# The order of the work behind the last unit of a Perceiver layer: quads taken two at a time

## The chip, the cores and the metric

The kernel runs on one core of a Trainium2 chip. The metric is the device time of one execution in microseconds. The profile used here was taken by the hardware profiler from one execution. PE is TensorE (PEld its weight loads), DVE is VectorE, ACT is ScalarE, POOL is GpSimd, and SP issues DMAs.

## The reference, cut to what matters

One Perceiver layer for 4 batches of 256 rows of width 256, all in float32: cross attention over a context of 4096 rows with 16 heads of 16, then a causal linear attention with random features, then a gated feed-forward network of width 768. Each of the three is added to x behind a layer norm. The change touches only the end of the program, where the linear attention and the feed-forward network of the later batches run:

```python
x = x + xattn(layernorm(x), ctx)
# attn: 16 heads of 16; features of q and k, 64 per head
feat = exp(clip(xn @ omega * sqrt(2 s) - s, -20, 20)) / sqrt(32) * sqrt(weight)
kv = cumsum(k_feat[t] outer v[t]); ks = cumsum(k_feat[t])          # over t, causal
out[t] = (q_feat[t] @ kv[t]) / max(q_feat[t] . ks[t], 1e-6)
x = x + out @ Wout + bout
# ffn
x = x + (silu(z @ wg.T) * (z @ wu.T)) @ wd.T                       # z = layernorm(x)
```

The kernel computes the causal sum as a masked product: scores of keys against queries with the part above the diagonal set to zero, then a product with V, which carries a column of ones, so that the same product gives the denominator. The result is divided by it.

## The kernel before

Heads are taken four at a time, a quad. There are 4 batches of 4 quads, numbered n = 0 to 15, with b = n // 4. The cross attention runs in units, one per quad, in a long loop that fills most of the time; the linear attention of quads 0 to 4 is spread through the last of these units by a plan. What is left stands behind the last unit, from about 1067 us on in the profile: quads 5 to 15 of the linear attention, the queries, keys and values of batch 3, the output projections of batches 1 to 3 and the feed-forward network of all four batches.

For each quad, `attend(n)` gives three pieces. In this document they have the names that the new code gives them:

- masked(n) is `scores()`: for each of two halves, four products with weights of 64 x 128 (lines 327 and 332) into two PSUM tiles `pa`. The two tiles of the first half are copied by ACT (L338) and masked by POOL (L339); those of the second half are masked by DVE while it copies (L344). The results are four tiles `at`.
- valued(n) is `values()`: eight products with weights of 128 x 32 (L353) into one tile `po`, which ACT copies to `avT` (L359).
- divided(n), for an odd n, is `divide()`: four transposes of the two last `avT` into `pt_o` (L369), and on DVE the reciprocal of the denominators and the quotient (L374 to L376).

The other pieces are: `features(n)`, for an even n, which makes the features of quads n and n + 1 (16 product instructions into four `pf` tiles, L301; for each a clip on DVE, L307, an exponential on ACT, L308, and a scaling on POOL, L309); `hidden(b, m)`, a third of the gated hidden layer of batch b (`pg` and `pu`, L575; tanh on ACT, L579; two DVE steps, L580 and L581); `down(b, i)`, its second product (`pd`, L591), with the sum and the store of the output; `outputs[b]`, two pieces, the transposes `tr_o` with their copy (L393, L394) and the projection `py` (L401); `norm(b)` and `turn(b)`, the layer norm ahead of the feed-forward network and its transposes; `norm3`, `turn3`, `qk3`, `v3` and `sq3`, the same and the projections for batch 3 of the linear attention; `ends`, the small DVE steps of the norms of its queries and keys; `qk_normed` and `qk_turned`, which scale and transpose these; and `divide15` and `project15`, the division and the projection for the last unit of the cross attention. `load_root` and the end of `norm` change the function table of ACT between square root and tanh.

Each bank of PSUM is one tile of a pool with `bufs=8`, so that a product waits until a bank has been read out. The tiles `at` have 8 buffers and `avT` three.

PE, ACT, DVE and SP run in the order in which the program issues their instructions (`tc.manual_schedule`); POOL's order is left to the scheduler. So the order in which the pieces are called is the order on each of those four engines. Before, a loop over n sets it: it calls the product with V of the quad before, then the masked products of quad n, then the pieces of a table `first`, then for an even n the division of the pair before, then the pieces of a table `fills`. A quad's masked products thus stand right behind the product with V of the quad before, and the other work between quad n's masked products and its product with V.

Of the kernel before, what the change touches and what calls it, by code (L numbers as in the profile page):

```python
# [26 lines left out]
NQ = H // 4  # L27
# [7 lines left out]
NH = HID // P  # L35
# [4 lines left out]
def perceiver_layer(  # L40
# [160 lines left out]
    def bank(shape, name):  # L201

        return psum.tile(shape, F32, tag="b", name=name)
# [60 lines left out]
    def normed_pieces(tiles):  # L264

        some = nrm[:, tiles[0] : tiles[-1] + 1, :].rearrange("p t h -> p (t h)")
        made = []

        def clipped():
            nc.vector.tensor_scalar(some, some, 1e-24, None, ALU.max)  # L270
            y, (first, *others) = inverse_root(some)
            made.extend([*others, lambda: nc.vector.tensor_copy(some, y)])
            first()

        return [clipped] + 4 * [lambda: made.pop(0)()]
# [13 lines left out]
    def feature(n, part):  # L289
        i = 2 * (n % 4) + part  # L290
        return kts[2 if n % 8 < 4 else 0][:, i * 2 * T : (i + 1) * 2 * T]
# [21 lines left out]
    def attend(n, scalar=True):  # L313

        b, q = divmod(n, NQ)
        ats = []

        def scores():  # L320
            for part in range(2):
                f = feature(n, part)
                qf, kf = f[:, :T], f[:, T:]
                pas = [bank([P, 3, P], "pa") for _ in range(2)]
                for j, pa in enumerate(pas):
                    rows = slice(64 * j, 64 * j + 64)
                    nc.tensor.matmul(  # L327
                        pa[:, 0:2, :], lhsT=kf[rows, :P], rhs=qf[rows, :], start=True, stop=True
                    )
                for j, pa in enumerate(pas):  # L330
                    rows = slice(64 * j, 64 * j + 64)
                    nc.tensor.matmul(  # L332
                        pa[:, 2, :], lhsT=kf[rows, P:], rhs=qf[rows, P:], start=True, stop=True
                    )
                for pa in pas:
                    at = place["at"]()
                    if part == 0 and scalar:
                        nc.scalar.copy(at, pa)  # L338
                        nc.gpsimd.affine_select(  # L339
                            out=at[:, 0:3:2, :], in_=at[:, 0:3:2, :], compare_op=ALU.is_ge, fill=0.0, base=0,  # L340
                            pattern=[[0, 2], [1, P]], channel_multiplier=-1,
                        )
                    else:
                        nc.vector.tensor_tensor(at, pa, place["mask"], ALU.mult)  # L344
                    ats.append(at)

        def values():
            po = bank([P, T], "po")
            for i in range(2):
                for j, at in enumerate(ats):  # L350
                    c0 = (4 * q + j) * (HD + 1)
                    rhs = at[:, 2, :] if i else at[:, 0:2, :]
                    nc.tensor.matmul(  # L353
                        po[32 * j : 32 * j + 32, i * P : T], lhsT=va[:, 2 * b + i, c0 : c0 + 32], rhs=rhs,
                        start=i == 0, stop=i == 1,
                    )
            if scalar:
                oT = place["avT"]()
                nc.scalar.copy(oT, po)  # L359
            else:  # L360
                oT = lnp.tile([P, T], F32, tag="avT4", name="avT4", bufs=1)
                nc.vector.tensor_copy(oT, po)
            got.append(oT)

        def divide():
            pt = bank([P, 2, 8, 32], "pt_o")
            for m, oT in enumerate(got):
                for i in range(2):
                    nc.tensor.transpose(  # L369
                        pt[:, i, 4 * m : 4 * m + 4].rearrange("p j r -> p (j r)"), oT[:, i * P : (i + 1) * P], ident  # L370
                    )
            got.clear()
            den = lnp.tile([P, 2, 8], F32, tag="den", name="den")
            nc.vector.tensor_scalar(den, pt[:, :, :, HD], 1e-6, None, ALU.max)  # L374
            nc.vector.reciprocal(den, den)
            nc.vector.tensor_tensor(  # L376
                place["att"](b)[:, :, 64 * q - 64 : 64 * q + 64].rearrange("p t (j d) -> p t j d", d=HD),
                pt[:, :, :, :HD], den.unsqueeze(3).to_broadcast([P, 2, 8, HD]), ALU.mult,
            )

        return scores, values, divide

    def output(b):

        tiles = (2 * b, 2 * b + 1)
        oTs = []

        def turn():
            for t in tiles:
                oT = place["oT"]()  # L390
                ps = bank([P, KC, P], "tr_o")
                for k in range(KC):
                    nc.tensor.transpose(ps[:, k, :], place["att"](b)[:, t % 2, k * P : (k + 1) * P], ident)  # L393
                nc.scalar.copy(oT, ps)  # L394
                oTs.append(oT)

        def project():
            for t, oT in zip(tiles, oTs):
                py = bank([P, D], "py")
                for k in range(KC):  # L400
                    nc.tensor.matmul(py, lhsT=oT[:, k, :], rhs=rest[8][:, k, :], start=k == 0, stop=k == KC - 1)  # L401
                nc.vector.tensor_tensor(xr[:, t, :], py, xr[:, t, :], ALU.add)

        return turn, project
# [197 lines left out]
    with tc.manual_schedule(engines={ET.PE, ET.Activation, ET.DVE, ET.SP}):  # L602
        *divide15, project15 = finish
        NB = B * NQ
        norm3, turn3, qk3, sq3, v3, _ = causal_in(3, norm_late)
        ff = {0: feed_forward(0)}
        outputs = [output(b) for b in range(B)]
        ends = normed_pieces((6, 7))

        def call(f, *args):  # L610
            return lambda: f(*args)

        def norm(b):
            def begin():
                ff[b] = feed_forward(b)
                ff[b][0]()

            return begin

        def turn(b):  # L620
            return lambda: ff[b][1]()

        def hidden(b, m):
            return lambda: ff[b][2](m)

        def down(b, *args):
            return lambda: ff[b][3](*args)


        first = {  # L630
            6: divide15,
            8: [turn3],
            10: ends[2:] + [call(qk_normed, 6), call(qk_normed, 7)],
            13: [norm(2)],
        }
        fills = {
            4: [turn(0), call(features, 6)],
            5: [hidden(0, 0)],
            6: [call(features, 8), hidden(0, 1), project15, load_root],
            7: [norm3, hidden(0, 2)],  # L640
            8: [call(features, 10), call(qk3, 0), down(0, 0), outputs[1][0], call(qk3, 1), outputs[1][1], load_root],
            9: [norm(1), v3, call(sq3, 0), call(sq3, 1), down(0, 1), *ends[:2], turn(1)],
            10: [hidden(1, 0), call(qk_turned, 6), call(qk_turned, 7)],
            11: [call(features, 12), hidden(1, 1)],
            12: [hidden(1, 2), *outputs[2], load_root],
            13: [call(features, 14), down(1, 0), down(1, 1), turn(2)],
            14: [hidden(2, 0)],
            15: [hidden(2, 1)],
            16: [
                hidden(2, 2), *outputs[3], load_root, norm(3), down(2, 0), down(2, 1, range(3)), turn(3),  # L650
                down(2, 1, range(3, NH)), *[hidden(3, m) for m in range(NH // 2)], down(3, 0), down(3, 1),
            ],
        }
        steps = [attend(n) for n in range(NB)]
        for n in range(NQ, NB + 1):
            if n > NQ + 1:
                steps[n - 1][1]()
            if NQ < n < NB:
                steps[n][0]()
            for piece in first.get(n, []):  # L660
                piece()
            if n > NQ and n % 2 == 0:
                steps[n - 1][2]()
            for piece in fills[n]:
                piece()


def cross_attention(tc, xr, load_x, load_queries, load_rest, ctxT, wq_sb, bq_sb, bqu_sb, wkP, bk_sb, wvP, eps,
# [547 lines left out]
```

## Time and profile before

| | us |
|---|---|
| median of 3 runs | 1188.66 (1188.03 to 1188.67) |
| the profiled execution, its own time | 1187.94 |
| span of the profiled execution | 1186.2 |
| PE busy over the span | 1175.3 (99%) |
| DVE, ACT, POOL busy over the span | 905.9, 700.4, 231.1 |
| PE busy from 1067.26 to 1087.00 (19.74 us) | 19.74 |
| PE busy from 1107.00 to 1130.00 (23.00 us) | 23.00 |
| DVE, ACT busy in the same 23.00 us | 17.74, 10.97 |

The span goes from the first to the last instruction; the execution's own time also holds what lies around it. A matmul's end is modelled, so a busy PE is one that has work queued, not one at its peak. In the order of time, a line has its start, its length, the engine and source line, and in brackets how long the engine had been idle and who released it. In the chain of waits, a line has a start, a length and the group of work that the end of the kernel hung on there.

### The profile page before, as it was taken

How to read it: one execution, taken by the hardware profiler on the slowest of the kernel's cores; microseconds unless marked ns; L12 is line 12 of the kernel's file. 1: busy time of each engine (PE TensorE's matmuls, PEld its weight loads, DVE VectorE, ACT ScalarE, POOL GpSimd, SP SyncE). 2: the span in 40 equal slices, each digit the busy share in tenths (PEclk: the TensorE clock that was granted, in tenths of full speed). 3: DMA queues.
4: the chain of work that ended last, by engine and by line, in shares of the span. 5: the costliest groups of instructions: out<-in, count | busy, mean ns of one | idle time of the engine just before them, and what ended most of it. 6: DMA issues, size and time to landing. Idle time of an engine off the chain costs nothing.

```text
span 1186.2 us, 42993 instructions
## 1 busy us (share of the span) xinstructions
PE 1175.3 (99%) x18024; PEld 801.3 (68%) x18024; DVE 905.9 (76%) x1723; ACT 700.4 (59%) x1450; POOL 231.1 (19%) x437
## 2 busy tenths in 40 slices
PE   8999999999999999999999999999999999999998
PEld 5476667666776677667766776677666666667777
DVE  7987777877777787778777877798887789567653
ACT  4446666666665666566656656665665456876442
POOL 3730302021111112121202020203031221103210
PEclk9999999999999999999999999999999999999999
DMA  6562342144223422342224322432243120000000
GB/s 211 142 212 74 107 118 81 63 110 115 77 76 90 117 92 82 83 116 83 82 80 117 104 82 74 103 106 83 71 114 97 55 65 29 11 2 10 10 11 18
DMA packets 55161, 100.00 MB, mean 84 GB/s; under 512 B 23392, under 2 KB 28056, under 8 KB 54968
## 3 DMA queue, kind: packets, MB, share of 16 engines
q1 hardware_dynamic: 44904, 91.84, 26.2%
q0 software_dynamic: 9440, 4.81, 2.1%
q8 instruction: 143, 2.34, 0.8%
q10 hardware_dynamic: 624, 0.59, 0.2%
q14 instruction: 50, 0.41, 0.1%
HBM read 76.13 MB, written 3.21 MB: 67 GB/s over the span
## 4 chain that ended last, share of the span: by engine, by line
PE 97%; DVE 2%; ACT 0%; issue 0%; POOL 0%; ACTq 0%; DVEq 0%; POOLq 0%
PE pt L849 23%; PE pm L803 19%; PE pav L869 19%; PE pv L180 11%; PE pk L180 11%; PE pg L575 2%; PE pd L591 2%; PE pu L575 2%; PE pa L327 1%; PE pqk L180 1%; PE po L353 1%; DVE mx L810 1%; PE pf L301 1%; PE py L401 1%; PE py L180 1%; PE pa L332 1%
## 5 line engine op out<-in xcount | busy, mean ns | idle before, releaser
L854 ACT ACTIVATE e<-pt 128x512 f32<-128x512 f32 x1024 | 529.5, 604 | 375.0 <-PE pm L803 359.5
L810 DVE TENSOR_REDUCE mx<-pm 128x1 f32<-128x512 f32 x1024 | 635.0, 683 | 125.1 <-PE pm L803 124.8
L849 PE MATMUL pt<-qa,kt 32*128 32x256 f32 x4096 | 504.0, 388 | 0.7 <-DVE qa L835 0.5
L803 PE MATMUL pm<-kt,qT 32*128 32x512 f32 x2048 | 500.7, 617 | 0.4 <-ACT ln_rs L123 0.3
L849 PEld LDWEIGHTS pt<-qa,kt 32*128 32x128 f32 x4096 | 319.8, 184 | 124.2 <-ACT v L774 41.6
L869 PE MATMUL pav<-e,v 128*32 128x256 f32 x4096 | 269.1, 380 | 0.0
L803 PEld LDWEIGHTS pm<-kt,qT 32*128 32x128 f32 x2048 | 183.1, 191 | 17.0 <-DVE mx L810 4.9
L869 PEld LDWEIGHTS pav<-e,v 128*32 128x32 f32 x4096 | 128.3, 110 | 74.7 <-issue 5.1
L879 DVE TENSOR_TENSOR av<-pav,av 128x256 f32<-128x256 f32 x240 | 101.6, 423 | 56.5 <-PE pav L869 56.3
L180 PE MATMUL pv<-wv_sb,wff 128*32 128x128 f32 x4096 | 137.3, 276 | 0.0
L180 PE MATMUL pk<-wff,wk_sb 128*32 128x256 f32 x2048 | 136.8, 388 | 0.0
L180 PEld LDWEIGHTS pv<-wv_sb,wff 128*32 128x32 f32 x4096 | 104.3, 109 | 44.0 <-DVE mx L810 44.0
L180 PEld LDWEIGHTS pk<-wff,wk_sb 128*32 128x32 f32 x2048 | 54.8, 109 | 66.1 <-DVE mx L810 38.8
L918 POOL TENSOR_TENSOR oT<-oT,bvT 128x64 f32<-128x64 f32 x32 | 8.6, 288 | 390.8 <-DVE oT L915 389.2
L746 ACT ACTIVATE ku<-pk,bk_sb 128x256 f32<-128x256 f32 x128 | 63.3, 495 | 12.2 <-PE pk L180 12.1
L901 POOL DMA_DIRECT2D oT<-scr x112 | 66.4, 625 | 20.2 <-DMA scr<-av 17.1
L825 POOL DMA_DIRECT2D qa<-neg x60 | 33.1, 564 | 140.1 <-DVE neg L822 102.8
L774 ACT COPY v<-pv 128x256 f32<-128x256 f32 x128 | 51.7, 404 | 9.7 <-PE pv L180 9.7
L344 DVE TENSOR_TENSOR at<-pa,mask 128x384 f32<-128x384 f32 x34 | 17.3, 552 | 19.9 <-PE pa L332 19.9
L976 POOL DMA_DIRECT2D qT<-qu x56 | 26.8, 486 | 14.8 <-ACT qu L973 10.5
L308 ACT ACTIVATE kt<-kt,shift 128x512 f32<-128x512 f32 x32 | 22.3, 727 | 8.4 <-DVE kt L307 8.4
L307 DVE TENSOR_SCALAR kt<-pf,low,top 128x512 f32<-128x512 f32 x32 | 23.7, 803 | 4.4 <-PE pf L301 4.4
(146 smaller groups left out, 648.7 us busy)
## 6 DMA issues: line engine op xcount, KB each, us to landing
wff<-in_ctxT_dram SPq DMA_DIRECT2D x128, 512.0 KB
kt<-ku SPq DMA_DIRECT2D x510, 32.0 KB
scr<-av POOLq DMA_DIRECT2D x14, 128.0 KB, 2.0
oT<-scr POOLq DMA_DIRECT2D x112, 8.0 KB, 2.7
xr<-in_x_dram SPq DMA_DIRECT2D x4, 256.0 KB
out_dram<-o SPq DMA_DIRECT2D x8, 128.0 KB
qa<-neg POOLq DMA_DIRECT2D x60, 1.0 KB, 3.5
qT<-qu POOLq DMA_DIRECT2D x56, 16.0 KB, 3.5
```

The costliest lines, as they stand in the source:

```text
L180: nc.tensor.matmul(out[js], lhsT=lhsT[:, js], rhs=rhs, **flags)
L575: nc.tensor.matmul(ps[:, i, :], lhsT=w[:, k, ns], rhs=zT[:, k, :], start=k == 0, stop=k == KC - 1)
L746: nc.scalar.activation(ku[:, cs], made.pop(), AF.Identity, bias=bk_sb[:, m : m + 1])
L774: nc.scalar.copy(to.rearrange("p t (h d) -> p t h d", d=HD + 1)[:, :, :, :HD], made.pop().rearrange("p t (h d) -> p t h d", d=HD),)
L803: nc.tensor.matmul(pm, lhsT=qT[rows, q, ts], rhs=kt[rows, c * CH : (c + 1) * CH], start=True, stop=True,)
L810: nc.vector.tensor_reduce(mx[:, i, j, c : c + 1], pm, AX.X, ALU.max)
L825: nc.gpsimd.dma_start(out=qa[32 * j : 32 * j + 1, :].rearrange("o (p i) -> o p i", i=2), in_=neg[:, j, :])
L849: nc.tensor.matmul(pt[:, i, :], lhsT=kt[rows, ks], rhs=qa[rows, :], start=True, stop=True)
L854: nc.scalar.activation(e, pt, AF.Exp, scale=0.25)
L869: nc.tensor.matmul(pav[32 * h : 32 * h + 32, :], lhsT=v[:, t % KT, c0 : c0 + 32], rhs=es[n, h][:, i, :], start=i == 0, stop=i == 1,)
L879: nc.vector.tensor_tensor(avs[u], pav, avs[u], ALU.add)
L901: queue.dma_start(out=oT[:, k, q % 2, j], in_=scr[32 * j : 32 * j + HD, k * P : (k + 1) * P].rearrange("e (r a) -> r e a", a=16),)
```

## The change

The two tables and the loop go, and one list takes their place. From quad 6 on, the masked products of two quads are called on end, and so are the two products with V; the other pieces stand between them in one list.

```diff
-        first = {
-            6: divide15,
-            8: [turn3],
-            10: ends[2:] + [call(qk_normed, 6), call(qk_normed, 7)],
-            13: [norm(2)],
-        }
-        fills = {
-            4: [turn(0), call(features, 6)],
-            5: [hidden(0, 0)],
-            6: [call(features, 8), hidden(0, 1), project15, load_root],
-            7: [norm3, hidden(0, 2)],
-            8: [call(features, 10), call(qk3, 0), down(0, 0), outputs[1][0], call(qk3, 1), outputs[1][1], load_root],
-            9: [norm(1), v3, call(sq3, 0), call(sq3, 1), down(0, 1), *ends[:2], turn(1)],
-            10: [hidden(1, 0), call(qk_turned, 6), call(qk_turned, 7)],
-            11: [call(features, 12), hidden(1, 1)],
-            12: [hidden(1, 2), *outputs[2], load_root],
-            13: [call(features, 14), down(1, 0), down(1, 1), turn(2)],
-            14: [hidden(2, 0)],
-            15: [hidden(2, 1)],
-            16: [
-                hidden(2, 2), *outputs[3], load_root, norm(3), down(2, 0), down(2, 1, range(3)), turn(3),
-                down(2, 1, range(3, NH)), *[hidden(3, m) for m in range(NH // 2)], down(3, 0), down(3, 1),
-            ],
-        }
         steps = [attend(n) for n in range(NB)]
-        for n in range(NQ, NB + 1):
-            if n > NQ + 1:
-                steps[n - 1][1]()
-            if NQ < n < NB:
-                steps[n][0]()
-            for piece in first.get(n, []):
-                piece()
-            if n > NQ and n % 2 == 0:
-                steps[n - 1][2]()
-            for piece in fills[n]:
-                piece()
+
+        def masked(*quads):
+            return [steps[n][0] for n in quads]
+
+        def valued(*quads):
+            return [steps[n][1] for n in quads]
+
+        def divided(n):
+            return steps[n][2]
+
+
+        order = [
+            turn(0), call(features, 6), *masked(5), hidden(0, 0),
+            *valued(5), *masked(6, 7), *divide15, divided(5), call(features, 8), hidden(0, 1), project15, load_root,
+            norm3, hidden(0, 2),
+            *valued(6, 7), *masked(8, 9), turn3, divided(7), call(features, 10), call(qk3, 0), down(0, 0),
+            outputs[1][0], call(qk3, 1), outputs[1][1], load_root, norm(1), v3, call(sq3, 0), call(sq3, 1),
+            down(0, 1), *ends[:2], turn(1),
+            *valued(8, 9), *masked(10, 11), *ends[2:], call(qk_normed, 6), call(qk_normed, 7), divided(9),
+            hidden(1, 0), call(qk_turned, 6), call(qk_turned, 7), hidden(1, 1),
+            call(features, 12), *valued(10, 11), divided(11), hidden(1, 2), *masked(12, 13), *outputs[2], load_root,
+            norm(2), call(features, 14), down(1, 0), down(1, 1), turn(2),
+            *valued(12, 13), *masked(14, 15), divided(13), hidden(2, 0), hidden(2, 1),
+            *valued(14, 15), divided(15), hidden(2, 2), *outputs[3], load_root, norm(3), down(2, 0),
+            down(2, 1, range(3)), turn(3), down(2, 1, range(3, NH)), *[hidden(3, m) for m in range(NH // 2)],
+            down(3, 0), down(3, 1),
+        ]
+        for piece in order:
+            piece()
```

Besides the pairs, four things stand elsewhere than before. `hidden(1, 1)` is called ahead of `features(12)` and of the products with V of quads 10 and 11, not behind `features(12)` and ahead of valued(11). divided(11) follows valued(11) directly, where masked(12) stood between them. masked(12) and masked(13) follow `hidden(1, 2)`, and `outputs[2]` follows them. `hidden(2, 0)` and `hidden(2, 1)` are called one after the other, ahead of valued(14) and valued(15).

## The prediction

> **What bounds the kernel now.** I read the page's chain first, then the same chain cut to the end of the kernel, where the diff acts (from 1067 us on), then the order of time of ACT and DVE there.
>
> ```profile
> PE 97%; DVE 2%; ACT 0%; issue 0%; POOL 0%; ACTq 0%; DVEq 0%; POOLq 0%
> ```
>
> TensorE sets the end; every other engine has slack. Between 1067.26 and 1183 us the chain leaves PE three times only: at 1129.94, 1154.69 and 1159.26 (each about 0.4 us on an ACT copy, 0.2 to 0.3 us of it not covered). So a gap on PE is lost, and a us saved on PE is won. The chain of waits in the stretch of quads 6 and 7 (start, length, both in us):
>
> ```profile
> 1082.69 0.65 PE po L353 x16
> 1083.34 0.63 PE pa L327 x4
> 1083.97 0.22 PE pa L332 x4
> 1084.19 0.43 PE pa L327 x4
> 1084.63 0.22 PE pa L332 x4
> 1084.85 1.92 PE pg L575 x8
> 1086.77 1.73 PE pu L575 x8
> 1088.50 0.79 PE po L353 x16
> ```
>
> The same work has two prices. The first half of a quad's masked products costs 0.63 + 0.22, the second 0.43 + 0.22: 0.20 more where the shape of the weights goes from 128 x 32 to 64 x 128. The product with V costs 0.79 here, and 0.65 where it follows `py`, which also has 128 x 32 weights: 0.14. pg costs 1.92 behind pa and pu, of the same size, 1.73: 0.19. pt_o is 0.59 behind pa and 0.44 behind tr (at 1091.38): 0.15.
>
> Then the in-order queues. The order of time around features(12), the four exponentials that come with it, and the end of quad 15, which has no work between its product with V and its division:
>
> ```profile
> 1067.78 1.15 PE L301 MATMUL pf<-qT,om_sb 32*128 32x256 f32 x16
> 1068.94 2.97 DVE L307 TENSOR_SCALAR kt<-pf,low,top 128x512 f32<-128x512 f32 x4 [1.22 <-PE pf L301]
> 1069.79 2.88 ACT L308 ACTIVATE kt<-kt,shift 128x512 f32<-128x512 f32 x4 [1.20 <-DVE kt L307]
> ...
> 1120.59 2.88 ACT L308 ACTIVATE kt<-kt,shift 128x512 f32<-128x512 f32 x4 [1.65 <-DVE kt L307]
> 1123.37 0.58 ACT L579 ACTIVATE th<-pg 128x512 f32<-128x512 f32 x1
> 1124.23 0.37 ACT L359 COPY avT<-po 128x256 f32<-128x256 f32 x1 [0.28 <-PE po L353]
> ...
> 1154.71 0.37 ACT L359 COPY avT<-po 128x256 f32<-128x256 f32 x1 [1.95 <-PE po L353]
> 1155.13 0.20 PEld L369 LDWEIGHTS pt_o<-ident,avT 128*128 128x128 f32 x2 [0.36 <-ACT avT L359]
> ```
>
> From the start of pf to the first clip on DVE 1.16 us, from there to the first exponential 0.85, and ACT is free again 3.63 us after the first clip (1072.57 for features(6): its next copy). Before the change, this train of exponentials ran beside hidden(1,1) on PE; nobody on PE waited for it.
>
> [...] th at 1123.37 began when the exponentials let it, though its pg had been finished for 1.7 us. [...] the pool has bufs=8 with one tile per bank, so two quads' masked products (8 `pa`) take all of them.
>
> **The change, part by part.**
>
> *Fewer changes of shape on PE.* Count the groups that enter a new shape. Masked products: 11 entries (quads 5 to 15) become 6, since 7, 9, 11, 13, 15 follow another quad: 5 x 0.20 = 1.00. Groups with 128 x 32 weights: 14 (5 and 7 to 15 are ten, 6 merged with py1 as one, qk3 twice, v3) become 10 (5, py1, the five pairs, qk3 twice, v3): 4 x 0.14 = 0.56. Full-size groups: hidden(1,1) and hidden(2,1) now follow full-size work (2 x 0.19 saved), tr_o of outputs[2] now follows pa (0.15 lost): 0.23. The entries of pf stay five. Sum: 1.8 us off PE. No product is added or removed.
>
> *divided(11) directly behind valued(10, 11), and these behind features(12).* Before, masked(12) and hidden(1,1) stood between. Count from T, the start of pf of features(12). PE: pf 1.07, po 0.79, po 0.65: done at T + 2.51. ACT holds the four exponentials ahead of the two avT copies: first clip T + 1.09 (chain start; DVE is free, the last hT of hidden(1,1) takes it to T + 0.73), ACT free at T + 1.09 + 3.63 = T + 4.72, two copies of 0.37, the second 0.33 behind the first: T + 5.42. The second pair of pt_o transposes starts at T + 5.47 and the next pg 0.28 later (1155.13 to 1155.41 at quad 15): T + 5.75. Without the wait pg would start 0.50 behind po (1143.79 to 1144.29 at quad 13): T + 3.01. So 2.74 us of PE stand open, and queued behind pt_o is all of hidden(1,2). Bounds: if the exponentials were done by then, only the copy's 0.34 as at quad 15 (1155.41 less 1154.57, less 0.50); nothing makes it negative. I take 2.75.
>
> *masked(8, 9) behind hidden(0,2) and valued(6, 7).* Eight banks: quad 9 must get banks held by pg, pu of hidden(0,2), po of 6 and 7, or quad 8 itself. When are they free? DVE is pushed: the clips of features(8) start behind quad 7's evictions (1077.72 + 0.94), the division of unit 15 (0.99 to den) and den's part: 1080.69 instead of 1079.38. So exponentials end at 1084.40, th of hidden(0,1) ends 1084.88, STT and hT to 1086.4, the xr sum, the statistics of norm3 from 1086.65, the root at 1087.84 (1087.46 before), the table load of 1.28 and th of hidden(0,2) at 1089.56 to 1090.14. Then the avT copies: po 6 free at 1090.45, po 7 at 1090.78; on DVE pg at 1090.9, pu at 1091.69. PE reaches quad 9 at 1074.87 (quad 6's start, unchanged) + 1.50 (quad 6) + 1.30 (quad 7) + 0.59 (pt_o) + 1.07 (pf) + 3.65 (hidden(0,1)) + 1.00 (py1) + 3.65 (hidden(0,2)) + 1.44 (two po) + 1.50 (quad 8) = 1090.57. If the pool gives out the banks as they come free (po, po, pg, then quad 8's first copy at 1091.2), quad 9 loses 0.2 to 0.4 us; in order of allocation (pg, pu first) 1.15. Below nothing it cannot go. I take 0.3.
>
> *With one answer (nothing).* The other pairs: masked(6, 7), (10, 11), (12, 13), (14, 15) find the banks before them emptied at least 0.3 us before use (shortest: valued(8), copied 0.4 us behind). divided(5), (7), (9), (13) have a masked pair or more behind their copies. qk_normed(6, 7) moves behind four evictions instead of two and ends 0.6 us before qk_turned(6) is due; without that cover its delay would be PE's. norm(2) now starts right behind py of outputs[2], features(14) and eight pd products (5.4 us) cover its root, tables and exponentials. outputs[2] waits for its copy as before (0.24); divided(15) and outputs[3] too. load_root and norm3 now follow each other on ACT, counted above. No DMA is moved but the out stores, which nobody waits for; POOL's selections come earlier. A pair fills all eight `at` and two of three `avT`; their last readers are PE's products and transposes of the pair before, which stand ahead in PE's own queue.
>
> *Sum:* -1.8 + 2.75 + 0.3 = +1.25 us. The profiled execution took 1187.94 (span 1186.2); that is 0.7 below the median 1188.66 of the three runs shown, within 0.1 of their lowest. Added to the median: 1189.9. About 0.2%, 2.4 us, is what a measurement of this kernel can tell from no change, so this forecast counts as no change, on the slow side.
>
> **Rivals.**
>
> *Banks decide (slower).* One mechanism: quad 9 waits for its eighth bank. For it: th of hidden(0,2) stands behind a root, two table loads and two DVE steps, and quad 8's own DVE evictions come behind hT, 1092.2 and 1092.65. If the last bank is one of these, quad 9 loses 1.45 instead of 0.3: -1.8 + 2.75 + 1.45 = +2.4, 1191.1. It decides from a wait of 1.43 us. Against it: banks freed earlier exist.
>
> *The shape costs nothing by itself.* If the 0.20 came from operands that arrive late, the pairs save little, and +3.05 gives 1191.7. Against it: a quad's second half never shows it and po behind py doesn't either, with operands equally old.
>
> *The exponentials are covered.* If ACT gets ahead (avT copies not held), only 0.34 remains at quad 11, and -1.8 + 0.34 + 0.3 = -1.2, 1187.5; with no wait at all 1186.9. Against it: ACT's queue is in order, as th at 1123.37 shows. Even so it stays within 0.2%.
>
> **How the numbers follow.** Forecast 0.50 (its own range 1188.9 to 1190.8: the bank wait from 0 to 0.6, the saving 1.4 to 2.0), banks 0.25, shape free 0.08, covered 0.13, something not seen 0.04. Slower by over 0.2% (above 1191.0): 0.18 of the banks' chance, whose price is near the line and open upwards, 0.07 of the free shape, 0.08 of the forecast's own upper end, 0.02 unseen: 0.35. Faster by over 0.2% (below 1186.3): 0.05, since the shapes saved are worth 1.8 at most. Same: 0.60. The range goes from covered (1187.4) to beyond the free shape (1191.9).
>
> **What would show it.** In the chain after: pa groups of 0.43 at the second quad of each pair and second po of 0.65; one break at divided(11) of 2.7 us, with PE's pt_o waiting on avT L359 and ACT's L308 ahead of it; a short wait before quad 9's L327. Wrong if pt_o of quad 11 waits under 1 us, if the 0.20 remains at quads 7, 9, 11, 13, 15, or if another gap of over 1 us shows on PE.

## The result and the profile after

| | before | after |
|---|---|---|
| median of 10 runs, us | 1188.49 (1187.3 to 1190.05) | 1191.88 (1190.52 to 1193.36) |
| ratio to before, 95% interval | | 1.0027 (1.0018 to 1.0035) |
| the profiled execution, us | 1187.94 | 1190.52 |
| from the first tr_z to the last sum on DVE, us | 115.64 | 119.05 |

The changed kernel is slower, by about 3.2 us (2.1 to 4.2 by the interval). The last row is the stretch that the change can touch, read from the chain of waits: from the start of the first `tr_z L566` to the start of the last `o L597`. It is a better ruler than the whole execution. The instructions ahead of it are the same in all the kernels of this study, and yet the stretch begins anywhere between 1066.39 and 1069.47 us. Inside it, the change costs 119.05 - 115.64 = 3.41 us.

TensorE still sets the end. The chain of the changed kernel by engine:

```profile
PE 96%; DVE 2%; ACT 1%; DMA 0%; issue 0%; POOL 0%; DVEq 0%; ACTq 0%; POOLq 0%
```

It is now 96% instead of 97% PE. The chain of waits in order of time (start, length) shows where it leaves PE. First the pair of quads 8 and 9, then division 11:

```profile
1089.78 0.72 PE pa L327 x3
...
1091.80 0.59 PE tr L224 x4
...
1120.47 1.11 PE pf L301 x16
1121.59 0.80 DVE kt L307
...
1122.41 2.18 ACT kt L308 x4
...
1125.20 0.36 ACT avT L359
...
1125.60 0.71 PE pt_o L369 x4
1126.32 2.62 PE pg L575 x8
1128.93 2.53 PE pu L575 x8
```

Three readings. Quad 9 (from 1089.78) should take 1.30 us behind quad 8 (twice 0.43 + 0.22) and takes 2.02 to `tr` at 1091.80: 0.72 of wait. Second, the forecast chain is there piece for piece: pf, the clip on DVE, the exponentials on ACT, the avT copy, and only then pt_o. PE's products with V had ended at 1121.59 + 1.44 = 1123.03; pg would have started 0.59 later and starts at 1126.32: 2.70 us of gap. The third was not forecast: pg and pu of hidden(1,2) take 2.62 and 2.53 us where they took 1.73 each, with no wait in them. That is 1.70 us more for the same products. In the chain of before the same pieces are:

```profile
1126.26 1.73 PE pg L575 x8
1127.98 1.73 PE pu L575 x8
```

The busy time by stretch shows why. Columns are the stretch and its length, the busy time of PE, PEld, DVE, ACT and POOL with the number of instructions, and then the granted clock of TensorE (1.00 is full), the DMA share and GB/s:

```profile
1123.00:1125.60 2.60, 0.00 (x0) 0.00 (x0) 1.53 (x3) 2.60 (x6) 1.65 (x4) 1.00 0.00 0
1125.60:1126.40 0.80, 0.80 (x6) 0.70 (x7) 0.05 (x1) 0.22 (x1) 0.26 (x1) 1.00 0.00 0
...
1127.00:1128.00 1.00, 1.00 (x4) 0.80 (x3) 0.27 (x1) 0.00 (x0) 0.00 (x0) 0.51 0.00 0
...
1130.00:1130.50 0.50, 0.50 (x3) 0.40 (x2) 0.29 (x1) 0.00 (x0) 0.00 (x0) 0.58 0.00 0
1130.50:1131.40 0.90, 0.90 (x7) 0.52 (x5) 0.00 (x0) 0.00 (x0) 0.00 (x0) 1.00 0.00 0
```

PE is idle for 2.60 us and comes back at full clock; 1.4 us later the clock halves. From the shares 0.51 and 0.58 the slow stretch runs from about 1127.02 to 1130.42: 3.4 us at half speed, which is 1.70 us lost, just what pg and pu lost. In the kernel before the clock of the stretch from 1126 to 1130 us is 1.00:

```profile
1126.00:1130.00 4.00, 4.00 (x23) 3.45 (x21) 2.42 (x7) 0.63 (x2) 0.43 (x2) 1.00 0.00 0
```

This is not a matter of the profiled execution alone. The mean clock of the ten executions of after is 0.995 to 0.997, on average 0.996; that of 101 executions of before, taken beside the experiments, is 0.997 to 1.000, on average 0.998. One slow stretch is worth 1.70 us of 1188, 0.0014. What links the slow stretch to the gap is so far only that it follows it; e1 to e5 test that.

The account of the stretch: gap 2.70 + slow clock 1.70 + quad 9 0.72 = 5.12; the stretch grew by 3.41, so 1.71 us were saved elsewhere. This is a remainder. The chain of e2 below, which has after's order but for one exchange and has no such gap, gives the changes of shape directly, when its pieces are summed by tile and compared with before: `pa` 1.01 less (without the wait at quad 9), `po` 0.56 less, `pg` 0.38 less, `tr_o` 0.15 more, together 1.80. The other 0.09 are small differences of other pieces.

### The profile page after: what moved, and what is told of

The parts are those of the page before. It is cut to its first block, busy times and chain, and to the rows that moved or that the text cites. A ratio compares the mean times of both kernels' runs of the same rounds, so it can differ in the third digit from the quotient of the medians.

```text
span 1188.8 us, 43009 instructions
## 1 busy us (share of the span) xinstructions
PE 1175.0 (99%) x18024; PEld 802.4 (67%) x18024; DVE 906.4 (76%) x1723; ACT 700.5 (59%) x1450; POOL 231.1 (19%) x437
## 4 chain that ended last, share of the span: by engine, by line
PE 96%; DVE 2%; ACT 1%; DMA 0%; issue 0%; POOL 0%; DVEq 0%; ACTq 0%; POOLq 0%
PE pt L842 23%; PE pm L796 19%; PE pav L862 19%; PE pv L180 11%; PE pk L180 11%; PE pg L575 2%; PE pu L575 2%; PE pd L591 2%; PE pa L327 1%; PE pqk L180 1%; DVE mx L803 1%; PE po L353 1%; PE pf L301 1%; PE py L401 1%; PE pa L332 1%; PE py L180 1%
```

## The experiments

Theory: the time comes from the gap, the slow clock that the gap brings, and the banks at quad 9, less the changes of shape. Rival: the queue alone, and the slow clock has nothing to do with the gap. For every run the table has the ratio to before, taken on the same chip, with its interval, and the stretch from the first tr_z to the last sum in the profiled execution. The runs were on several chips, so their medians are compared through the ratios, and the stretches, one execution each, carry the differences of under 1 us.

| kernel | ratio to before | stretch, us |
|---|---|---|
| before | 1 | 115.64 |
| after | 1.0027 (1.0018 to 1.0035) | 119.05 |
| e1, division later | 1.0001 (0.9993 to 1.0010) | 114.67 |
| e2, values first | 0.9992 (0.9986 to 0.9999) | 114.62 |
| e3, gap filled | 1.0016 (1.0007 to 1.0025) | 117.37 |
| e4, gap alone | 1.0045 (1.0032 to 1.0057) | 120.55 |
| e5, gap half filled | 1.0014 (1.0007 to 1.0020) | 117.36 |
| e6, hidden first | 0.9991 (0.9983 to 1.0000) | 114.54 |
| e7, pairs interleaved | 0.9993 (0.9985 to 1.0002) | 115.40 |
| e8, all waits covered | 0.9981 (0.9974 to 0.9989) | 113.30 |
| e9, down first | 0.9968 (0.9957 to 0.9979) | 112.61 |

**e1: the division later.**

```diff
-            call(features, 12), *valued(10, 11), divided(11), hidden(1, 2), *masked(12, 13), *outputs[2], load_root,
+            call(features, 12), *valued(10, 11), hidden(1, 2), divided(11), *masked(12, 13), *outputs[2], load_root,
```

> After, with divided(11) moved behind hidden(1,2), so that 3.5 us of PE work cover the avT copies. Theory 'gap and clock': the change's 3.4 us over before are a gap of 2.7 us at divided(11), about 1.7 us or more because PE's clock falls after the gap, 0.7 us of bank waits at quad 9, less 1.7 us of shape changes. Both the gap and the slow stretch must go: 1188.5 - 1.7 + 0.7 = 1187.5 us, granted clock 1.00 in the stretch of hidden(1,2), pg L575 and pu L575 of 1.73 us there. Rival 'queue alone': the slow stretch has nothing to do with the gap; only 2.7 us go, 1191.9 - 2.7 = 1189.2 us, and some stretch near the end still shows a clock of 0.5.

Median 1187.57 us. The stretch loses 4.38 us against after, which is gap and slow clock together (2.70 + 1.70 = 4.40); pg and pu are 1.92 (with a change of shape) and 1.73, and the mean clock of the profiled execution is 1.000 (0.997 in after), so no slow stretch is left in it. The rival's 1189.2 would have been a ratio of 1.0006 and falls by the stretch, though the two ratios' intervals alone would not tell.

**e2: the values first.**

```diff
-            call(features, 12), *valued(10, 11), divided(11), hidden(1, 2), *masked(12, 13), *outputs[2], load_root,
+            *valued(10, 11), call(features, 12), divided(11), hidden(1, 2), *masked(12, 13), *outputs[2], load_root,
```

> After, with the products with V of quads 10 and 11 called ahead of features(12), so that their two copies stand ahead of the four exponentials on ACT. The pf group (1.07 us) covers them. 'Gap and clock': pt_o of quad 11 waits under 0.1 us, clock 1.00 there, 1187.5 us. If the masked products of quad 12 now wait for features(12), because only pt_o and hidden(1,2), 4 us, stand between, up to 0.5 us more. 'Queue alone': 1189.2 us.

Median 1187.1 us. Its chain there:

```profile
1120.43 1.44 PE po L353 x32
1121.86 1.08 PE pf L301 x16
1122.94 0.59 PE pt_o L369 x4
1123.53 1.73 PE pg L575 x8
```

The same four pieces, two of them exchanged, and PE is not left once. The 1.08 us of pf cover the two copies, which now stand ahead of the exponentials on ACT. The masked products of quad 12 did not wait for features(12). With this the idea of the pairs does what the shapes promise: 1.02 us less than before in the stretch (1.80 saved on shapes, 0.73 lost at quad 9, small differences elsewhere), ratio 0.9992.

**e3: the gap filled.** Six products are added that nobody reads; nothing is left out.

```diff
-            call(features, 12), *valued(10, 11), divided(11), hidden(1, 2), *masked(12, 13), *outputs[2], load_root,
+            call(features, 12), *valued(10, 11), busy(6), divided(11), hidden(1, 2), *masked(12, 13), *outputs[2], load_root,
```

> After, with six added products of 128x128 weights and 256 columns (about 2.6 us, into a bank that nobody reads) ahead of divided(11): the wait for the avT copies stays, but PE is busy in it. 'Gap and clock': hidden(1,2) runs at full clock, so the time falls to 1188.5 - 1.7 + 2.7 + 0.7 = 1190.2 us though work was added, pg and pu L575 of 1.73 us there. 'Queue alone': no change from after, 1191.9 us, or slightly more.

Median 1190.23 us: work was added and the kernel became faster than after, in the stretch by 1.68 us. (The ratios, 1.0016 and 1.0027, point the same way, but their intervals overlap.) The chain:

```profile
1123.15 2.79 PE busy L645 x12
1125.94 0.54 PE pt_o L369 x4
1126.48 1.73 PE pg L575 x8
```

pt_o comes even a little later behind the products with V (2.79 us; 2.57 in after), but hidden(1,2) runs at full speed, with a clock of 1.00 from 1126 to 1130 us. So the slow stretch is caused by PE's idleness and not by the lateness of pt_o. The rival falls.

**e4: the gap alone, in the kernel before.**

```diff
-            11: [call(features, 12), hidden(1, 1)],
-            12: [hidden(1, 2), *outputs[2], load_root],
+            11: [hidden(1, 1), call(features, 12)],
+            12: [*outputs[2], load_root],
...
+            if n == 12:
+                steps[11][2]()
+                hidden(1, 2)()
             if NQ < n < NB:
...
-            if n > NQ and n % 2 == 0:
+            if n > NQ and n % 2 == 0 and n != 12:
```

> Before, with the gap alone: hidden(1,1) ahead of features(12), then valued(11), divided(11) and hidden(1,2) directly, then masked(12); quads are not paired. The avT copy of quad 11 again stands behind the four exponentials: a gap of 3.1 us, and one change of shape more (0.15). 'Gap and clock': a slow stretch of clock behind it costs 1.7 us or more: 1188.5 + 3.2 + 1.7 = 1193.4 us, up to 1195. 'Queue alone': 1188.5 + 3.2 = 1191.7 us and clock 1.00 behind the gap.

Median 1193.41 us, and the stretch is 4.91 us longer than before, as forecast (3.2 + 1.7). No pairs are needed for it. The first two transposes, of quad 10, run before the gap, so PE is idle in one piece for 2.90 us, from 1126.14 to 1129.04. Busy time by stretch, columns as above:

```profile
1125.80:1129.00 3.20, 0.34 (x2) 0.10 (x2) 2.17 (x4) 3.13 (x5) 1.61 (x4) 1.00 0.00 0
1129.00:1129.70 0.70, 0.66 (x3) 0.66 (x4) 0.00 (x0) 0.00 (x0) 0.30 (x1) 0.50 0.00 0
1129.70:1130.70 1.00, 1.00 (x4) 0.81 (x3) 0.85 (x3) 0.00 (x0) 0.00 (x0) 0.50 0.00 0
```

Here PE comes back into the slow clock at once, where in after it had 1.4 us at full clock first. So the halving doesn't come at a fixed time after PE's return. Nor does it come at a fixed time after PE fell idle: 4.0 us in after (1123.03 to 1127.02), 2.9 in e4 (1126.14 to 1129.00). The length is the same: by the share of 0.67 in the stretch from 1131.70 to 1132.80, the slow clock of e4 ends at about 1132.43, after 3.4 us as in after:

```profile
1131.70:1132.80 1.10, 1.10 (x5) 0.93 (x4) 0.00 (x0) 0.00 (x0) 0.00 (x0) 0.67 0.00 0
```

What sets the moment of the halving was not shown.

**e5: the gap half filled,** with `busy(3)` in place of `busy(6)`.

> As the kernel with the gap filled, but with three added products instead of six: PE is busy for 1.4 us of the wait and idle for about 1.3. [...] 1190.2 us as with the gap filled, clock 1.00 in hidden(1,2). If any gap of over 1 us starts the slow stretch: 1191.9 us as after, pg L575 over 2 us there.

Median 1190.05 us, the stretch 117.36 as with the whole gap filled (117.37). PE in order of time:

```profile
1125.46 1.56 PE L645 MATMUL busy<-wff,ident 128*128 128x256 f32 x6
1128.14 0.71 PE L369 MATMUL pt_o<-ident,avT 128*128 128x128 f32 x4 [1.12 <-ACT avT L359]
```

1.12 us of idleness did not slow the clock:

```profile
1128.10:1130.00 1.90, 1.85 (x11) 1.63 (x12) 0.85 (x3) 0.26 (x1) 0.30 (x1) 1.00 0.00 0
```

So of the gaps ahead of pt_o in these runs, those of 2.60 us (after) and 2.90 us (e4) were followed by half the clock, and that of 1.12 us was not. No run shows what lies between.

**e6: hidden(0,2) ahead of project15,** on e2.

```diff
-            *valued(5), *masked(6, 7), *divide15, divided(5), call(features, 8), hidden(0, 1), project15, load_root,
-            norm3, hidden(0, 2),
+            *valued(5), *masked(6, 7), *divide15, divided(5), call(features, 8), hidden(0, 1), hidden(0, 2), project15, load_root,
+            norm3,
```

> The kernel with values first (1187.1 us), with hidden(0,2) moved ahead of project15, so that its tanh stands ahead of the square root and the table loads on ACT and pg and pu are read out earlier. If the 0.7 us at quad 9 are a wait for the banks of pg, pu and po behind that tanh, they fall to 0.2 or less, and two changes of shape go (0.33): 1187.1 - 0.8 = 1186.3 us. If the wait has another cause it stays 0.7 and only 0.3 us go: 1186.8 us.

A miss: 1187.08 us, the stretch only 0.08 us shorter than e2's. The two changes of shape went, as the chain shows (the second pg at 1.73, po behind py1 at 1.30), but quad 9 waited longer than before: from 1092.47 to `tr` at 1094.75 it took 2.28 us, 0.98 of them wait, where e2 had 0.73. The 0.25 took back most of what the two changes of shape gave (0.34). That is neither of the two cases of the forecast. The chain at quad 9:

```profile
1092.47 0.43 PE pa L327 x4
...
1093.15 0.36 ACT avT L359
...
1094.75 0.58 PE tr L224 x4
```

ACT, DVE and PE in order of time:

```profile
1089.30 0.69 DVE L581 TENSOR_TENSOR hT<-pu,th 128x512 f32<-128x512 f32 x1
1091.74 1.28 ACT L550 ACT_TABLE_LOAD   x1
1093.15 0.63 ACT L359 COPY avT<-po 128x256 f32<-128x256 f32 x2
1093.65 0.88 PE L327 MATMUL pa<-kt 64*128 64x256 f32 x4 [0.52 <-ACT avT L359]
```

pg and pu are read out by 1089.99, 2.5 us before quad 9 begins. What is late now are the two copies that free the banks of po: they stand behind the table load on ACT. It is still a wait for a bank, but the last one to come free is another. I had moved one of two things that stand behind the table.

**e7: the pairs interleaved,** on e2, at three places (quads 6 to 9, 8 to 11, 12 to 15).

```diff
-            *valued(6, 7), *masked(8, 9), turn3, divided(7), call(features, 10), call(qk3, 0), down(0, 0),
+            *valued(6), *masked(8), *valued(7), *masked(9), turn3, divided(7), call(features, 10), call(qk3, 0), down(0, 0),
```

> The kernel with values first (1187.1 us), with the order value, masked, value, masked instead of two values and two masked at quads 6 to 9, 8 to 11 and 12 to 15. Nothing else moves; six groups more begin with a change of shape. If a change costs what the trace of before shows, 3 x (0.20 + 0.14) = 1.0 us more, of which up to 0.3 is hidden in the bank wait at quad 9: 1187.8 to 1188.1 us. If the shape is free by itself: 1187.1 us or less.

Median 1187.77 us; the stretch is 0.78 us longer than e2's. Six groups more begin with a change of shape, 1.02 us by the prices of the trace of before. Quad 9's own wait falls from 0.73 to 0.49 us, since PE comes to it later. 1.02 - 0.24 = 0.78. So the price of the shape change stands, measured by itself in the stretch; the ratios alone (0.9993 against 0.9992) could not show it.

**e8: three more waits covered,** on e6.

```diff
-            *valued(10, 11), call(features, 12), divided(11), hidden(1, 2), *masked(12, 13), *outputs[2], load_root,
+            *valued(10, 11), call(features, 12), divided(11), hidden(1, 2), outputs[2][0], *masked(12, 13), outputs[2][1], load_root,
...
-            *valued(12, 13), *masked(14, 15), divided(13), hidden(2, 0), hidden(2, 1),
-            *valued(14, 15), divided(15), hidden(2, 2), *outputs[3], load_root, norm(3), down(2, 0),
+            *valued(12, 13), *masked(14, 15), divided(13), hidden(2, 0), *valued(14, 15), hidden(2, 1),
+            divided(15), hidden(2, 2), outputs[3][0], down(2, 0, range(1)), outputs[3][1], load_root, norm(3),
+            down(2, 0, range(1, NH)),
```

> The kernel with hidden(0,2) ahead of project15, with three more waits covered: the transposes of outputs[2] ahead of masked(12, 13), valued(14, 15) ahead of hidden(2,1), and one of the six pd steps of down(2,0) between the transposes and the projection of outputs[3]. By the waits of the trace (0.24, 0.34, 0.24) about 0.75 us less than that kernel: 1185.6 us, ratio to before 0.998. If what is taken from one wait returns at another, no change from it.

Median 1185.99 us. The stretch is 1.24 us shorter than e6's, more than the 0.75 forecast, and nothing of it returned elsewhere. By the chains of the two, the division gave 0.35 and each of the two projections some 0.45: from tr_o on, outputs[3] took 0.23 + 0.44 + 1.99 = 2.66 us in e6, and 0.44 + 1.80 in e8. py behind a break is 0.19 longer by itself, which the forecast had not counted.

**e9: down(0,0) ahead of the values of quads 6 and 7,** on e8.

```diff
-            norm3,
-            *valued(6, 7), *masked(8, 9), turn3, divided(7), call(features, 10), call(qk3, 0), down(0, 0),
+            norm3, down(0, 0),
+            *valued(6, 7), *masked(8, 9), turn3, divided(7), call(features, 10), call(qk3, 0),
```

> The kernel with all waits covered, with down(0,0), 2.6 us of PE work, moved ahead of valued(6, 7). With hidden(0,2) moved, quad 9 still waited 0.7 us, now for the two avT copies behind the table load. If that is a wait for the banks of po, quad 9's products come 2.6 us later and wait no more: 0.7 us less, two changes of shape more (0.33), so about 0.4 us less from the first transposes to the last sum (113.3 us there), 112.9 us. If the stretch without down(0,0) between features(10) and outputs[1] now makes the projection wait for its copies behind the exponentials, the 0.4 us are given back or more, and PE's py L401 waits there.

Median 1184.39 us. The stretch is 112.61 (113.3 in e8; 112.9 forecast). The chain at quads 8 and 9:

```profile
1090.21 1.44 PE po L353 x32
1091.65 0.63 PE pa L327 x4
...
1093.16 0.43 PE pa L327 x4
...
1094.47 0.59 PE tr L224 x4
```

Quad 9 begins at 1093.16 and takes 1.31 us to `tr`, without a wait, so it was the banks. The wait was 0.98 us in e8 as in e6, not the 0.7 of the forecast. Less two changes of shape (`po` 0.14, `tr_o` 0.15) this gives the 0.69 won. The projection did not come to wait: py takes 1.93 us, right behind pqk. This kernel is faster than both others: 0.9968 (0.9957 to 0.9979) of before. The stretch explains 3.03 us of it.

## Why the prediction came out as it did

The time lay in the range, by luck: 1191.88 is at its upper end, 1191.9, which had been set for changes of shape that cost nothing, and these do cost. Two of the three terms were right. The likeliest case was wrong all the same: it said +1.25 us, within 0.2%, and the kernel is slower by 0.27% (0.18 to 0.35), over the upper end of that case's own range (1190.8).

- *Changes of shape, -1.8 us:* 1.80 by the pieces of e2's chain, and e7 found the price of the single change again.
- *The gap at divided(11), 2.75 us:* 2.70, with the copies behind the exponentials on ACT as worked out, and e4 made it without the pairs. That hidden(1,2) queues behind pt_o was said too. The step that failed is the price put on it: the gap was charged with its own length and nothing more, as if PE came back as it had left. The 1.70 us of slow clock have no term in the sum, and no rival or range end was worked out for them. This was the one place where the change left PE idle for over 2 us (2.60), so it was the place to ask what happens behind such a gap.
- *The banks at quad 9, 0.3 us:* 0.72, over its own range of 0 to 0.6. The wait for a bank was right, and so were the times: counted from the first `tr_z`, PE came to quad 9 at 23.34 us (forecast 23.31) and hT ended at 24.39 (forecast 24.43). The step that failed is the choice of the bank. The 0.3 rested on a pool that gives out banks as they come free, so that the last of quad 9's four products would get the bank of quad 8's first copy:

```profile
1089.73 0.88 ACT L338 COPY at<-pa 128x384 f32<-128x384 f32 x2
1090.14 0.69 DVE L581 TENSOR_TENSOR hT<-pu,th 128x512 f32<-128x512 f32 x1
1090.88 0.18 PEld L327 LDWEIGHTS pa<-kt 64*128 64x128 f32 x1
```

Both copies of quad 8 on ACT were over at 1090.61, yet that product's weights were loaded only at 1090.88, right behind hT, which reads pu and ends at 1090.83. By these times the bank was pu's, the one that the worked-out case of 1.15 us named. That the loss was 0.72 and not 1.15 fits with the part of quad 9 that ran before it.

- *The rest at nothing:* right. The chain shows no wait at the pairs (6, 7), (10, 11), (12, 13) and (14, 15), and divided(15), outputs[2] and outputs[3] wait as they did.
- *The rivals:* the banks did not decide: 0.72 is under the 1.43 set for them. The free shape falls with e7. The covered exponentials fall with the chain of after, and e2 shows what that case is worth when the order makes it true.

1.25 + 1.70 (slow clock) + 0.42 (banks) - 0.05 (gap) = 3.32, against 3.41 measured in the stretch.

## What to carry to other kernels

When an order is rewritten for one engine, walk each wait back through the in-order queue of the engine that ends it: two 0.37 us copies cost 2.7 us because four exponentials had been called one line earlier. A gap on TensorE like those of 2.60 and 2.90 us here is to be priced twice, its length and what the clock does after it (here 1.70 us); filling it with useless products is a cheap test of that. And a wait for a bank goes only when the last bank goes (in e6 pg and pu were read out 2.5 us before quad 9, and it waited 0.98 us): list all that stand behind the same late instruction before moving one.

## What had not been expected of the hardware

After 2.60 us without a product, TensorE's granted clock stood at 0.50 for 3.4 us, starting 1.4 us after its return in one kernel and at once in another with a gap of 2.90 us; 1.12 us of idleness (e5) and the waits of 0.2 to 0.7 us elsewhere in after did not bring it (clock 1.00 from 1066.44 to 1127.00 and from 1130.43 to 1180.00 us).

The start of the program has such a stretch too. In the traces of before and after PE is idle for 2.78 us ahead of the first `tr` at 9.73 us, and the clock is 0.50 from 10.79 to 14.20 us in before and from 10.85 to 14.27 us in after, about 1.1 us behind PE's return and for 3.4 us. Not every execution has it: in the first 20 us the clock was 0.91 in the profiled executions of before, after and e2 and 1.00 in that of e8, and whether PE has the same gap in e8 was not shown. So the mean clock of one execution (0.995 to 1.000) does not show the gap at divided(11); the clock of the stretch does, or the mean over many executions.
